# Attention scores in a fixed order, PSUM pools kept open and normalization on ScalarE in a graph network kernel

## The chip, the cores and the metric

The kernel runs on one core of a Trainium2 chip. A core has five engines with queues of their own: TensorE (PE in the profile; its weight loads are PEld), VectorE (DVE), ScalarE (ACT), GpSimd (POOL) and SyncE (SP, which issues most of the DMAs). They meet only through semaphores. The metric is the device time of one execution in microseconds (us); the kernel before takes 974.41 us in the median of three executions (973.85 to 975.27).

## The reference

Two graph layers run over 625 nodes with 1024 features and 20000 edges, everything in float32. The edge list says for each edge its source, its destination and one of 8 types. Cut to what matters:

```python
# layer 0: attention
h = x @ W                                           # 625 x 1024 x 1024
al, ar = h @ a_l, h @ a_r
e = exp(-leaky_relu(al[src] + ar[dst], 0.1))
rowsum = segment_sum(e, src)
h_prime = segment_sum(e[:, None] * h[dst], src) / (rowsum[:, None] + 1e-5)
x = layernorm(x + elu(h_prime))                     # called x1 below
# layer 1: a relational graph network
u = x @ root + bias
for r in range(8):
    mask = edge_type == r
    mean = segment_sum(x[src] * mask, dst) / max(segment_sum(mask, dst), 1)
    u = u + mean @ weight[r]
z = concat([u, x]) @ w_gate + b_gate
x = layernorm(x + tanh(u) * z + x * (1 - z))
```

## The kernel before

**Tiles.** The nodes lie in 5 tiles of 125 rows (`ST`, `TN`). The 1024 features are 8 chunks of 128 (`KC`) where they are summed over, and two halves of 512 columns (`HALF`) where they are produced; one bank of PSUM, the memory that TensorE writes to, is used as 128 rows of 512 float32, and the kernel uses 8 banks.

**The stages**, with the time of each in the profile. First (to 101 us) h = x @ W (ph, L782), while the edges are turned into a dense count matrix for each type: VectorE builds one-hot tiles (L808), TensorE multiplies them (pc, L832), and ScalarE casts the counts (L837) into cj, one tile of source nodes j after the other. From DRAM the counts come back later, type by type (cd, cs, cf).

From about 101 to 140 us the attention scores are made. For a tile j, `all_types` adds the counts of the 8 types (c, L845, L847, L849). `scores_of` makes e = exp(-leaky_relu(al + ar)) times the count: L865 adds, L868 multiplies by 1 where there is an edge, L869 is the leaky ReLU, L870 the exp on ScalarE, L871 the product with the count, L872 the row sum. `turn_scores` transposes e on TensorE (patt, L883) and copies it to attT (L885), the weights of the matrix product with h (phh, L684), which `gather_h` issues and which sums over all five j.

After that (to 167.6 us) `attend` takes each finished row tile of phh: ELU by three operations on ScalarE (L1068 to L1070) and two on VectorE (L1072, L1073), the statistics (L1076, L978), the reciprocal standard deviation on GpSimd (L980 adds the epsilon, L981 is the power) and the normalization on VectorE (L1078). The normalized x1 goes to DRAM, and `turned_pieces` transposes it (px, L673).

**Dense products in pieces.** Every large product after that runs in float32r (0.227 us from one matmul of 128x512 to the next, against 0.86 for one in float32), on three pieces per operand that together carry float32's digits: `prepare` splits a chunk of weights into g, e (ScalarE, L998, L999), m and the final e (VectorE, L1000, L1001); `pieces_of` splits the turned activations into h (ScalarE, L1009), l and d (VectorE, L1010, L1011). A row tile of a half is 24 matmuls: g with h (L1025) and m with l (L1026) into bank p1, e with d (L1029) into bank p2. Ten buffers (`UNITS`) hold prepared chunks: the 8 of the present half and two of the next. The tiles of a half come one after the other; only tile 0 goes chunk by chunk through all three products, the others first through L1025 and L1026 and then through L1029.

These halves follow each other: root0 (167.6 to 197.7 us), root1 (to 227.06), 16 halves of `weight` (to 844.7, each followed by the product with the counts, pu L1195), and the gate: wgx0, wgx1 (x1's part of w_gate), wgu0, wgu1 (u's part), with u transposed in `turn_u` (L1223) during wgx1, to 960.4 us; then the last normalization and the output. root's sums are added to u by two operations on VectorE (L1112, L1113); u was loaded with the bias beforehand, by ten DMAs of 256 KB. The in-degrees per type, which divide the sums, are added up after root0 (L1134, L1136) and transposed on TensorE (p_ins, L1140).

**What sets the order.** The program gives the work in one order, and a scheduler that plans each engine's queue ahead of time may move an instruction past others where the data allow it. `tc.keep_in_program_order` pins an instruction behind the instruction that its engine was given before. The kernel before doesn't pin the scores. It makes each score depend on the one before it: L874 writes a 1 that comes out of the row sum of score j (`turn`), and L868 of score j + 1 takes that 1 as an operand. PSUM comes from pools: before the scores one of 6 and one of 2 banks, which are closed (`begin.close()`) and replaced by one of 8.

## Time and profile before

| quantity | value |
|---|---|
| median of three executions | 974.41 us (973.85 to 975.27) |
| the profiled execution's own time | 973.86 us |
| its span (first to last instruction) | 972.1 us |
| granted TensorE clock, mean | 0.992 |
| TensorE busy | 945.3 us (97%) |
| VectorE busy | 597.2 us (61%) |
| ScalarE busy | 391.4 us (40%) |
| 101 to 140 us: TensorE busy, granted clock | 31.00 of 39.00 us, 0.91 |
| 101 to 140 us: VectorE busy | 38.05 of 39.00 us |
| 227.1 to 844.7 us: TensorE busy | 617.60 of 617.60 us |
| 931.5 to 960.4 us (wgu1): TensorE busy | 27.92 of 28.90 us |

A line of the timeline gives the start, the length, the engine, the line of the kernel, the output and inputs, the number of records, and in brackets how long the engine had been idle before it and whom it waited for. A line of the waits gives the waiting instruction, the one that released it, the total in us, how often, and the longest. A line of the windows gives the stretch, its length, and for TensorE, its weight loads, VectorE, ScalarE and GpSimd the busy time and the records; then the granted clock, the share of the DMA engines' time and GB/s. A line of the groups gives line, engine, operation, output, inputs, shapes and count, then the total busy time in us and the mean of one in ns, and the idle time ahead of it with its releaser. A float32 matmul has two records.

### The profile page before, as it was taken

The numbers are of one execution on the slowest core, as the hardware profiler recorded it, in microseconds if no ns is written. First come the engines' busy times: TensorE is split into PE (matmuls) and PEld (weight loads), VectorE is DVE, ScalarE is ACT, GpSimd is POOL, SyncE is SP. The second block draws the span as 40 slices with busy tenths as digits, with TensorE's granted clock in tenths as the row PEclk, the third lists the DMA queues.
The fourth block names the chain that finished last, engine by engine and source line by source line (L and its number), as shares of the span: only waits on it lengthen the run. The fifth ranks groups of instructions, "written<-read, shape, count | busy, mean of one in ns | idle before, by whom it ended". The sixth has DMA issues, their size and how long they took to land.

```text
span 972.1 us, 10853 instructions
## 1 busy us (share of the span) xinstructions
PE 945.3 (97%) x4075; PEld 730.5 (75%) x4075; DVE 597.2 (61%) x960; ACT 391.4 (40%) x714; POOL 39.5 (4%) x69
## 2 busy tenths in 40 slices
PE   7999699999999999999999999999999999999995
PEld 3555445878888888888888888888888888888874
DVE  1998978976626546356265364562653644639995
ACT  1333837244434515515434345244342551433422
POOL 3000001000000000000000000000000000002123
PEclk9999999999999999999999999999999999999998
DMA  8134862442103113021122120320320211432213
GB/s 298 44 78 102 198 197 75 141 155 87 65 22 121 45 42 108 21 80 66 55 87 63 59 87 23 99 76 11 121 66 22 87 37 50 139 112 74 87 39 112
DMA packets 61631, 83.89 MB, mean 86 GB/s; under 512 B 29323, under 2 KB 29735, under 8 KB 61572
## 3 DMA queue, kind: packets, MB, share of 16 engines
q1 hardware_dynamic: 61364, 82.93, 27.6%
q8 instruction: 34, 0.56, 0.2%
q14 instruction: 25, 0.20, 0.1%
q0 software_dynamic: 208, 0.19, 0.1%
HBM read 71.36 MB, written 11.75 MB: 86 GB/s over the span
## 4 chain that ended last, share of the span: by engine, by line
PE 92%; DVE 5%; ACT 1%; DMA 1%; SPq 0%; issue 0%; POOL 0%; POOLq 0%; DVEq 0%; ACTq 0%
PE pu L1195 19%; PE p_w L1026 15%; PE p_w L1025 15%; PE p_w L1029 15%; PE ph L782 7%; PE phh L684 3%; PE p_root L1029 2%; PE p_root L1025 2%; PE p_wgx L1029 2%; PE p_wgx L1026 2%; PE p_wgx L1025 2%; PE p_root L1026 2%; PE pc L832 2%; PE p_wgu L1029 1%; PE p_wgu L1026 1%; PE p_wgu L1025 1%
## 5 line engine op out<-in xcount | busy, mean ns | idle before, releaser
L1026 PE MATMUL p_w<-m_w,x_l 128*128 128x512 f32 x640 | 249.1, 389 | 0.0
L1025 PE MATMUL p_w<-g_w,x_h 128*128 128x512 f32 x640 | 249.0, 389 | 0.0
L1195 PE MATMUL pu<-y,cf 125*128 125x512 f32 x800 | 184.4, 389 | 0.0
L1177 DVE SCALAR_TENSOR_TENSOR v<-p_w,v 125x512 f32<-125x512 f32 x80 | 55.2, 690 | 201.7 <-PE p_w L1029 153.0
L1029 PE MATMUL p_w<-e_w,x_d 128*128 128x512 f32 x640 | 176.4, 389 | 0.0
L1195 PEld LDWEIGHTS pu<-y,cf 125*128 125x128 f32 x800 | 150.2, 188 | 31.6
L1029 PEld LDWEIGHTS p_w<-e_w,x_d 128*128 128x128 f32 x640 | 120.1, 188 | 25.5 <-DVE e_w L1001 0.3
L1025 PEld LDWEIGHTS p_w<-g_w,x_h 128*128 128x128 f32 x640 | 120.2, 188 | 25.1
L1026 PEld LDWEIGHTS p_w<-m_w,x_l 128*128 128x128 f32 x640 | 120.1, 188 | 25.1 <-DVE m_w L1000 0.2
L1176 ACT ACTIVATE v<-p_w 125x512 f32<-125x512 f32 x80 | 47.6, 595 | 214.0 <-PE p_w L1026 214.0
L1000 DVE SCALAR_TENSOR_TENSOR m_w<-raw_w,e_w 128x512 fp32r<-128x512 f32 x128 | 84.9, 684 | 36.3 <-ACT e_w L999 36.3
L1180 DVE TENSOR_TENSOR y<-v,y 125x512 fp32r<-125x512 f32 x80 | 55.3, 691 | 50.8 <-ACT y L1179 50.8
L998 ACT ACTIVATE g_w<-raw_w 128x512 fp32r<-128x512 f32 x128 | 73.2, 621 | 29.8 <-PE p_w L1025 20.7
L1001 DVE TENSOR_TENSOR e_w<-g_w,m_w 128x512 fp32r<-128x512 f32 x128 | 84.9, 684 | 0.5
L1179 ACT CAST y<-v 125x512 fp32r<-125x512 f32 x80 | 49.2, 615 | 75.1 <-DVE v L1177 75.1
L782 PE MATMUL ph<-w,xT 128*125 128x512 f32 x160 | 77.6, 612 | 0.3 <-ACT xT L714 0.3
L999 ACT ACTIVATE e_w<-raw_w 128x512 fp32r<-128x512 f32 x128 | 73.2, 623 | 0.0
L1199 DVE SCALAR_TENSOR_TENSOR L_gnn_bias_dram_u<-pu,inv,L_gnn_bias_dram_u 125x512 f32<-125x512 f32 x80 | 55.5, 743 | 0.5
L1161 ACT CAST cf<-cs 128x640 fp32r<-128x640 f16 x40 | 25.9, 724 | 54.8 <-PE pu L1195 46.2
L1242 POOL TENSOR_TENSOR L_gnn_bias_dram_u<-L_gnn_bias_dram_u,xr 125x512 f32<-125x512 f32 x10 | 17.4, 1743 | 744.2 <-ACT L_gnn_bias_dram_u L1227 712.0
L684 PE MATMUL phh<-h_sb,attT 125*125 125x512 f32 x100 | 45.9, 614 | 0.4 <-ACT attT L885 0.4
L782 PEld LDWEIGHTS ph<-w,xT 128*125 128x125 f32 x160 | 27.9, 192 | 24.1 <-issue 22.2
(159 smaller groups left out, 972.0 us busy)
## 6 DMA issues: line engine op xcount, KB each, us to landing
raw_w<-in_L_gnn_weight_dram SPq DMA_DIRECT2D x64, 512.0 KB
cd<-cj SPq DMA_DIRECT2D x40, 160.0 KB
cs<-cd SPq DMA_DIRECT2D x8, 800.0 KB
x<-in_x_dram SPq DMA_DIRECT2D x8, 512.0 KB
w<-in_L_gnn_W_dram SPq DMA_DIRECT2D x8, 512.0 KB
raw_root<-in_L_gnn_root_dram SPq DMA_DIRECT2D x8, 512.0 KB
raw_wgx<-in_L_gnn_w_gate_dram SPq DMA_DIRECT2D x8, 512.0 KB
raw_wgu<-in_L_gnn_w_gate_dram SPq DMA_DIRECT2D x8, 512.0 KB
```

Source lines behind the costliest of these rows:

```text
L684: nc.tensor.matmul(banks_h[t, half][:n, :], attT[:nj, j, tile_cols(t)], h_sb[:nj, j, half * HALF:(half + 1) * HALF], start=(j == 0), stop= ...
L782: nc.tensor.matmul(p[:n, :], xT[:, k, :n], w0_sb[k][:, half * HALF:(half + 1) * HALF], start=k == 0, stop=k == KC - 1)
L998: nc.scalar.activation(g, w, AF.Copy, scale=DOWN)
L999: nc.scalar.activation(e, w, AF.Copy, scale=UP12 * DOWN)
L1000: nc.vector.scalar_tensor_tensor(m, w, UP12, e.bitcast(F32), op0=OP.mult, op1=OP.subtract)
L1001: nc.vector.tensor_tensor(e, g.bitcast(F32), m.bitcast(F32), op=OP.subtract)
L1025: nc.tensor.matmul(p1, h[:, k, :], g, start=k == 0, stop=False, skip_group_check=True)
L1026: nc.tensor.matmul(p1, l[:, k, :], m, start=False, stop=k == KC - 1, skip_group_check=True)
L1029: nc.tensor.matmul(p2, d[:, k, :], e, start=k == 0, stop=k == KC - 1, skip_group_check=True)
L1180: nc.vector.tensor_tensor(lo[:n], v[:n], hi[:n].bitcast(F32), op=OP.subtract)
L1195: nc.tensor.matmul(p, c[:m, t, j * 128:(j + 1) * 128], piece[:m], start=(t == 0 and i == 0), stop=(t == ST - 1 and i == 1), skip_group_che ...
L1199: nc.vector.scalar_tensor_tensor(at, p[:n], inv[:n, j, r:r + 1], at, op0=OP.mult, op1=OP.add)
```

## The change

- The scores are pinned on VectorE (`in_turn`) in an order that the program gives; `turn` is gone. `scores_of` is split, so that the product with the counts (`times_edges`) and the row sum (`sum_scores`) have places of their own. Scores 0 and 1 are begun in `first_scores` as soon as al and ar are there. The types of tiles 3 and 4 are added between the scores, and the copy of score 0's transposes lies on VectorE. The m pieces of root's first 8 chunks are pinned behind the scores.
- Two PSUM pools of 6 and 2 banks stay open for the whole kernel. A bank that names no pool takes them in turn, six and two; `begin.close()` is gone. patt and the phh of tile 3 name the pool of 2; px of x, p_count, p_edges, pc and p_ar that of 6.
- x1 is normalized on ScalarE: a [125, 1] operation on VectorE (-mean), one on ScalarE (times the reciprocal deviation) and one Identity over 1024 columns with both as pointers. The epsilon is added on VectorE, not on GpSimd. px of x1's tile 0 is issued after two of the five phh of tile 4.
- `dense_tiles` takes the last two row tiles of a half together, chunk by chunk, in root0, root1, wgx0, wgx1 and wgu0 (`goes_on`).
- root's p1 is evicted on ScalarE into u, and p2 added on VectorE. The ten bias loads are gone; the bias is added in relation 1, by five adds on VectorE after one load of 256 KB per half.
- The in-degrees are added in float16, in place of iota, and turned after root1 by five float16 matmuls with a float16 identity; one operation on VectorE takes the place of five. Relation 0's counts are loaded and cast after root1.
- `turn_u` of u's tiles 3 and 4 moves from wgx1 to wgu0, behind its tiles 0 and 1.

Where the diff shows only added lines, the lines that they replace are in the listing above.

```diff
...
     rawp = ctx.enter_context(tc.tile_pool(name="f_raw", bufs=4, side="right"))
-    begin = ExitStack()
-    ps = [begin.enter_context(tc.tile_pool(name="f_ps0", bufs=6, space=bass.MemoryType.PSUM))]
-    ps_h = begin.enter_context(tc.tile_pool(name="f_ps_h", bufs=2, space=bass.MemoryType.PSUM))
-    def bank(name):
-        return ps[0].tile([128, 512], F32, tag="bank", name=name)
+    ps = [ctx.enter_context(tc.tile_pool(name=f"f_ps{n}", bufs=n, space=bass.MemoryType.PSUM)) for n in (6, 2)]
+    turns = []
+    def bank(name, pool=None):
+        if pool is None:
+            pool = len(turns) % 8 // 6
+            turns.append(name)
+        return ps[pool].tile([128, 512], F32, tag="bank", name=name)
+    def in_turn(ins):
+        tc.keep_in_program_order(ins)
...
+        def all_types(j, part, put=lambda ins: None):
...
+            if part == 0:
+                c4 = attp.tile([128, ST, 4, 128], F16, name="c4")[:, :, :, :n]
+                fours.append(c4)
+                put(nc.vector.tensor_tensor(c4, cjs[j][:, :, 0:4, :n], cjs[j][:, :, 4:8, :n], op=OP.add))
+                return
+            c4 = fours.pop()
...
+            c1 = attp.tile([128, ST, 128], F16, name=f"c1_{j}")[:, :, :n]
+            ct.append(c1)
+            put(nc.vector.tensor_tensor(c2, c2, c4[:, :, 2:4, :], op=OP.add))
+            put(nc.vector.tensor_tensor(c1, c2[:, :, 0, :], c2[:, :, 1, :], op=OP.add))
...
+        def scores_of(j, parts=(0, 1)):
...
+            if 0 in parts:
+                e = attp.tile([128, ST, 128], F32, name=f"e_{j}")[:, :, :n]
+                es.append(e)
+                in_turn(nc.vector.tensor_tensor(
+                    e, ar_b[:, j * 128:j * 128 + n].unsqueeze(1).to_broadcast([128, ST, n]),
+                    al.unsqueeze(2).to_broadcast([128, ST, n]), op=OP.add))
+                in_turn(nc.vector.scalar_tensor_tensor(e, ct[j], 1.0, e, op0=OP.min, op1=OP.mult))
+            if 1 in parts:
+                in_turn(nc.vector.scalar_tensor_tensor(es[j], es[j], SLOPE, es[j], op0=OP.mult, op1=OP.max))
+                nc.scalar.activation(es[j], es[j], AF.Exp, scale=-1.0)
+        def times_edges(j):
+            in_turn(nc.vector.tensor_tensor(es[j], es[j], ct[j], op=OP.mult))
+        def sum_scores(j):
+            in_turn(nc.vector.tensor_reduce(rsum[:, :, j], es[j], axis=AX.X, op=OP.add))
...
+                p = bank(f"patt_{j}_{t0}", 1)
...
+                if j:
+                    nc.scalar.copy(attT[:n, j, c0:c1], p[:n, :c1 - c0])
+                else:
+                    in_turn(nc.vector.tensor_copy(attT[:n, j, c0:c1], p[:n, :c1 - c0]))
...
         def counted(j):
-            all_types(j, cjs[j])
+            if j < ST - 2:
+                all_types(j, 0)
+                all_types(j, 1)
...
+        def first_scores(_):
+            spread_ar()
+            scores_of(0)
+            scores_of(1, parts=(0,))
+            times_edges(0)
+            scores_of(1, parts=(1,))
...
                     if steps == n_steps:
-                        due.append((i + 6, lambda _: spread_ar(), None))
-                        due.extend((max(i + 6 + 4 * j, (j + 1) * NG + LAG), lambda _: es.append(scores_of(len(es))), None)
-                                   for j in range(AHEAD))
+                        due.append((i + 6, first_scores, None))
...
+            sum_scores(j)
             if j + 1 < ST:
+                later_types = j + 3 if j < 2 else None
+                if later_types:
+                    all_types(later_types, 0, in_turn)
+                times_edges(j + 1)
+                if later_types:
+                    all_types(later_types, 1, in_turn)
+                if j + 2 < ST:
+                    scores_of(j + 2)
...
         rstd = small.tile([128, 1], F32, name="rstd")
-        nc.gpsimd.tensor_scalar(rstd[:n], mv[:n, 1:2], EPS, None, op0=OP.add)
+        nc.vector.tensor_scalar(rstd[:n], mv[:n, 1:2], EPS, None, op0=OP.add)
...
             nc.scalar.activation(e, w, AF.Copy, scale=UP12 * DOWN)
-            nc.vector.scalar_tensor_tensor(m, w, UP12, e.bitcast(F32), op0=OP.mult, op1=OP.subtract)
+            rest = nc.vector.scalar_tensor_tensor(m, w, UP12, e.bitcast(F32), op0=OP.mult, op1=OP.subtract)
+            if pinned:
+                in_turn(rest)
...
+    def dense_tiles(ts, chunks, name, by_chunk):
+        sums = {t: (bank(f"p1_{name}_{t}"), bank(f"p2_{name}_{t}")) for t in ts}
+        def first(t, k, g, m):
+            h, l, _ = x1[t]
+            nc.tensor.matmul(sums[t][0], h[:, k, :], g, start=k == 0, stop=False, skip_group_check=True)
+            nc.tensor.matmul(sums[t][0], l[:, k, :], m, start=False, stop=k == KC - 1, skip_group_check=True)
+        def second(t, k, e):
+            nc.tensor.matmul(sums[t][1], x1[t][2][:, k, :], e, start=k == 0, stop=k == KC - 1, skip_group_check=True)
...
+            for t in ts:
+                first(t, k, g, m)
+                if by_chunk:
+                    second(t, k, e)
+        if not by_chunk:
...
+                for t in ts:
+                    second(t, k, e)
+        return sums
+    def dense(name, put, after=None, goes_on=False, whole=False):
...
+        steps = [(t,) for t in range(ST - 2)] + ([(ST - 2, ST - 1)] if goes_on else [(ST - 2,), (ST - 1,)])
+        for ts in steps:
+            for t, (p1, p2) in dense_tiles(ts, chunks, name, ts[0] == 0 or len(ts) > 1).items():
+                n = 128 if whole else rows_of(t)
+                put(t, p1[:n, :], p2[:n, :])
+                if t == 1:
+                    prepare(UNITS - KC)
+                if after:
+                    after(t)
...
         mv, rstd = rstd_of(stats, n)
-        nc.vector.tensor_scalar(x_t[:n], x_t[:n], mv[:n, 0:1], rstd[:n], op0=OP.subtract, op1=OP.mult)
+        shift = small.tile([128, 1], F32, name="shift")
+        nc.vector.tensor_scalar(shift[:n], mv[:n, 0:1], -1.0, None, op0=OP.mult)
+        nc.scalar.activation(shift[:n], shift[:n], AF.Copy, scale=rstd[:n])
+        nc.scalar.activation(x_t[:n], x_t[:n], AF.Identity, scale=rstd[:n], bias=shift[:n])
...
-    prepare(KC)
+    prepare(KC, pinned=True)
...
     done = [attend(0)]
-    turned_pieces(done[0], 0, "x1")
...
         gather_h(EARLY + 1, j)
+        if j == 1:
+            turned_pieces(done[0], 0, "x1")
...
     l1p = ctx.enter_context(tc.tile_pool(name="f_l1", bufs=1))
-    u = start_rows(l1p, bias, ("u0", "u1"))
+    u = [[l1p.tile([128, HALF], F32, tag=f"u{h}_{t}", name=f"u{h}_{t}") for h in range(2)] for t in range(ST)]
...
+    def start_u(h):
+        def put(t, p1, p2):
+            at = u[t][h]
+            nc.scalar.activation(at, p1, AF.Copy, scale=1.0 + EPS12)
+            nc.vector.scalar_tensor_tensor(at, p2, -EPS12, at, op0=OP.mult, op1=OP.add)
+        return put
...
-    dense("root0", add_to(u, 0), after=later_x1)
+    dense("root0", start_u(0), after=later_x1, goes_on=True, whole=True)
...
+    ins = iota16[:R]
+    ident16 = src2.rearrange("p b g h w -> p (b g h w)")[:R, :R]
+    def add_ins():
+        nc.vector.tensor_copy(ident16, ident[:R, :R])
+        nc.vector.tensor_tensor(ins, ins16[:, 0, :], ins16[:, 1, :], op=OP.add)
+        for t in range(2, ST):
+            nc.vector.tensor_tensor(ins, ins16[:, t, :], ins, op=OP.add)
+    in_p = yp.tile([TN, 1], F32, name="in_p")
+    def use_ins():
+        p = bank("p_ins")
+        for t in range(ST):
+            nc.tensor.matmul(p[:TN, t * R:(t + 1) * R], ins[:, t * 128:t * 128 + TN], ident16, start=True, stop=True)
+        p = p[:TN, :ST * R]
+        nc.vector.tensor_scalar(inv[:TN].rearrange("p t r -> p (t r)"), p, 1.0, None, op0=OP.max)
+        nc.vector.reciprocal(inv, inv)
+        nc.vector.tensor_reduce(in_p, p, axis=AX.X, op=OP.add)
+    def sum_ins():
+        p = bank("p_all")
+        nc.tensor.matmul(p[:1, :1], in_p, ones[:TN, :1], start=True, stop=True)
+        nc.vector.tensor_scalar(astray, p[:1, :1], -1.0, float(E), op0=OP.mult, op1=OP.add)
...
+    dense("root1", start_u(1), goes_on=True, whole=True)
+    add_ins()
+    use_ins()
...
     cast_counts(0)
-    dense("root1", add_to(u, 1))
...
-            dense(f"w{r}_{h}", put)
+            dense(f"w{r}_{h}", put, after=lambda t: (r, h, t) == (0, 0, 1) and sum_ins())
...
+                    if r == 1:
+                        nc.vector.tensor_tensor(at, at, bias_row[:n], op=OP.add)
+            if r == 1:
+                bias_row = l1p.tile([128, HALF], F32, tag="v", name=f"bias_{h}", bufs=2)
+                nc.sync.dma_start(bias_row, bass.AP(tensor=bias.tensor, offset=bias.offset + h * HALF,
+                                                    ap=[[0, 128], [1, HALF]]))
...
-    dense("wgx0", add_to(z, 0))
-    dense("wgx1", add_to(z, 1), after=turn_u)
-    dense("wgu0", mix(0))
+    dense("wgx0", add_to(z, 0), goes_on=True)
+    dense("wgx1", add_to(z, 1), after=lambda t: t < ST - 2 and turn_u(t), goes_on=True)
+    dense("wgu0", mix(0), after=lambda t: t < 2 and turn_u(t + ST - 2), goes_on=True)
```

## The prediction

> **What bounds the kernel now.** I read the page's totals and chain first, then the waits of TensorE, then its timeline and the windows where it is not full.
>
> ```profile
> span 972.1 us, 10853 instructions
> PE 945.3 (97%) x4075; PEld 730.5 (75%) x4075; DVE 597.2 (61%) x960; ACT 391.4 (40%) x714; POOL 39.5 (4%) x69
> PE 92%; DVE 5%; ACT 1%; DMA 1%; SPq 0%; issue 0%; POOL 0%; POOLq 0%; DVEq 0%; ACTq 0%
> ...
> PE patt L883 <- DVE e L871: 7.6, 3, 4.9
> PE p_wgu L1029 <- DVE e_wgu L1001: 1.0, 2, 0.6
> PE phh L684 <- ACT attT L885: 0.4, 1, 0.4
> ```
>
> TensorE is busy for 97%, so only its idle or slow stretches can be won. The largest wait that this change touches is that of patt (the turned scores): three times, 7.6 us, longest 4.9. The timeline of TensorE and four windows of 10 us show the place:
>
> ```profile
> 104.09 4.92 PE L832 MATMUL pc<-m_hot,s_hot 128*128 128x240 f16 x42
> 111.51 0.78 PE L883 MATMUL patt<-ident,e 125*125 125x125 f32 x5 [2.50 <-DVE e L871]
> 112.69 1.98 PE L684 MATMUL phh<-h_sb,attT 125*125 125x512 f32 x4 [0.40 <-ACT attT L885]
> 119.56 1.41 PE L883 MATMUL patt<-ident,e 125*125 125x125 f32 x5 [4.89 <-DVE e L871]
> 120.76 7.22 PE L684 MATMUL phh<-h_sb,attT 125*125 125x512 f32 x12
> 128.36 5.32 PE L684 MATMUL phh<-h_sb,attT 125*125 125x512 f32 x12
> 139.58 0.78 PE L883 MATMUL patt<-ident,e 125*125 125x125 f32 x5 [0.21 <-DVE e L871]
> ...
> 100.00:110.00 10.00, 9.01 (x75) 6.66 (x73) 9.12 (x15) 9.66 (x22) 0.00 (x0) 1.00 0.73 186
> 110.00:120.00 10.00, 3.20 (x11) 1.73 (x12) 10.00 (x15) 9.97 (x21) 0.95 (x1) 0.89 0.83 172
> 120.00:130.00 10.00, 10.00 (x26) 5.05 (x26) 10.00 (x19) 4.86 (x10) 0.00 (x0) 0.77 0.90 289
> 130.00:140.00 10.00, 9.79 (x30) 4.56 (x29) 9.93 (x17) 2.20 (x4) 0.00 (x0) 1.00 0.63 197
> ```
>
> From 110 to 140 VectorE (third busy figure) is full, while TensorE idles 2.50 + 0.40 + 4.89 + 0.21 = 8.0 us. A second loss: the granted clock falls to 0.77, and the same 12 records take 7.06 us, from 120.76 to the next patt at 127.82, against 5.15 later; with patt's 1.20 against 0.54 that is 2.6 us. VectorE is full because 20 operations on root's pieces stand between the scores: these two rows, 10 of each from 117.5 to 138.6, at one per 0.60 us, so 12.0 us.
>
> ```profile
> L1001 DVE TENSOR_TENSOR e_root<-g_root,m_root 128x512 fp32r<-128x512 f32 x16 | 10.8, 688 | 0.0
> L1000 DVE SCALAR_TENSOR_TENSOR m_root<-raw_root,e_root 128x512 fp32r<-128x512 f32 x16 | 10.5, 688 | 0.2 <-ACT e_root L999 0.2
> ...
> L1078 DVE TENSOR_SCALAR x<-x,mv,rstd 125x1024 f32<-125x1024 f32 x5 | 4.1, 812 | 3.8 <-POOL rstd L981 3.8
> L1266 ACT ACTIVATE gnn_b_gate_dram_y<-gnn_b_gate_dram_y,shift,rstd 125x512 f32<-125x512 f32 x8 | 6.1, 808 | 22.5 <-POOL shift L1262 22.5
> ...
> 930.00:940.00 10.00, 9.63 (x43) 7.34 (x42) 9.80 (x16) 3.24 (x6) 3.14 (x2) 1.00 0.14 46
> 940.00:950.00 10.00, 9.39 (x42) 7.45 (x41) 9.43 (x16) 0.63 (x1) 2.95 (x6) 1.00 0.09 27
> ```
>
> The last two lines are the gate stage: VectorE above 94%, TensorE short by 1.0 us. Between 227.06 and 844.7 TensorE is full in every window: nothing to win there.
>
> **1. Scores in fixed order.** A score costs VectorE five operations of 0.72 to 0.87, ScalarE an exp of 0.73. The fixed order puts root's pieces behind the last score. The types' sum of node tile j=3 (1.38 + 0.72 + 0.40 = 2.5 us) moves in between, so VectorE saves 12.0 - 2.5 = 9.5 us there. Walked operation by operation with these durations, 0.12 us from engine to engine: ar_b is copied by 104.6 as before; score 0 leaves its lrelu at 107.3, exp 108.1 (behind ScalarE's casts), product 109.7. patt 0 starts at 109.8, 0.8 after the last pc (109.01), not 2.5. Its copy now lies on VectorE, where it is next in line: phh from 111.1. Product 1 is ready at 114.15 and TensorE comes for it at 114.56; product 2 at 120.7 against 121.1; product 3 at 126.08, a stall of 0.24; product 4 at 130.1. So patt 4 starts at 130.3, not 139.58: **-9.3 us**. The same phh lie ahead of it in both orders. The margins are 0.3 to 0.4 us, so this term is -6 if each product is some 0.8 us later than walked, and -9.6 at best, when the stall of 0.24 goes too. The clock's 2.6 us is inside the 9.3: the longest idle left is about 0.8, and the trace's 0.40 and 0.21 are followed by nothing slow.
>
> The Trainium skill, "TensorE: Matmul & The Clock Gate", section "HAM oscillation", says that idle gaps above about 3.4 us halve the clock; the row agrees (4.89 idle, then 0.77), and by it as by the rows the short gaps left keep the full clock.
>
> **2. From x1 to root0.** Root's 16 pinned pieces now follow the scores, from 131 to 146 on VectorE, and the other 4 among the attends. phh takes 17.2 us as before, px 0 is due at 151.4. x1's path grows: rstd's add on VectorE (0.17, the row of the 125x1 operations) for POOL's 0.31, pow 0.57, two operations on ScalarE instead of one on VectorE. The 1024-wide Identity is not in the trace: at least 0.81 (the 512-wide row above), at most 1.62 (twice). I take 1.2: attT's copies give 0.47 at 375 columns and 0.37 at 250, 0.8 ns a column, so 0.81 + 0.4. Queued behind it on ScalarE are the next tile's q and m, and behind those VectorE's adds. By the walk x_0 is ready at 150.0 for px 0 at 151.4; x_3 at 168.6 for 170.1; x_4 at 175.0 for 176.4. Before, x_3 and x_4 had 8.4 and 3.3 us. So **0**, with 0.7 to 1.4 us of cover; gone, each px costs its lateness, together 0 to +4.
>
> The Trainium skill, "ScalarE: Activation LUTs", section "Rules for kernel authors", speaks against the move: add and mul belong on VectorE. The rows give 0.81 there and an estimated 1.2 here, but VectorE is the busier engine (8.4 to 9.7 of 10 from 150 to 190, ScalarE 1.7 to 7.1). By the page's rule each tile would be 0.4 later, all inside its cover; by the rows VectorE gains 5 x 0.72 us.
>
> **3. The last two tiles together.** In root0 the pair begins at 177.25 and asks for l_4 0.9 later; by the walk VectorE has it at 179.3: **+1.15**, between 0 and +3. In the gate stage each chunk is freed 1.36 us after the previous one during the last 10.9 us, instead of all in the last 5.4, so the next half's pieces are ready before it starts. The four halves take 115.7 us (844.72 to 960.4), against 113.2 for 20 tiles of 24 matmuls at 0.227 us and five turns of 0.87. Of the excess 2.4 (1.7 of it in wgu1) I take **-1.8**; 0 to -2.4 if it works, up to +3 if the eight operations of u's last two turns, now in wgu0, crowd VectorE: u_4's pieces are walked ready 12 to 17 us into wgu0, asked for at 18.1.
>
> **4. In-degree sums.** root1 takes 29.3 us from 197.73 to 227.06 with p_ins (5 x 0.33 by its neighbours' starts) and p_all between, against 27.2 for 120 matmuls of 0.227. fp16 needs one pass: 0.6 at the end, p_all goes under w0. **-1.2**, between 0 and -1.8.
>
> **5. At nothing.** Ten bias loads of 256 KB leave SP's queue at 167 to 172.5, where only x1's stores and weight loads stand behind them; two return in r=1. Ten adds of 0.60 in r=1 lie under 38.6 us halves in which VectorE is 55 to 60% busy. Evicting p1 on ScalarE frees 0.6 per tile; nobody waits for it while a bank is free. Two pools of 6 and 2 banks rotate as one of 8 did: 0, or up to +2 if phh waits for a bank. Tail: rstd's add off POOL, **-0.2**.
>
> **Sum.** -9.3 + 1.15 - 1.8 - 1.2 - 0.2 = -11.35 on the profiled 973.86 (span 972.1 and 1.8 around it): 962.5. The median 974.41 stands 0.55 above that run, so 963.0. A measurement here can tell about 0.2% (2 us) from no change.
>
> **Rivals.** (a) *VectorE just misses.* It is full from 105 to 180 and the covers are 0.3 to 1.4 us; if they fail, scores give -7 and px and the joint tiles cost +2.5 more: 968. For it: the thin margins. Against: the rows repeat within 1%. (b) *The gate stage turns worse*, +3 instead of -1.8: 968. For it: VectorE at 94 to 98%. Against: the work per half is the same. (c) *Nothing comes of it*: the scores are held by something other than VectorE's order, such as ScalarE, 9.97 busy from 110 to 120: 974. Against: its 4.86 and 2.20 after. (d) *Slower: x1's path through ScalarE.* m, q and Identity wait in one queue, each behind VectorE's adds, and five px wait for it in turn. It decides when each is over 2.5 us late beyond its cover (5 x 2.65 outweighs 11.35 and 2 us): that is four more ScalarE operations of 0.6 to 0.7 ahead of each. At 3.2 us each: +16 - 11.35, 979. For it: q waits for x on VectorE for 3.0 us already. Against: in root0 ScalarE is 17 to 22% busy.
>
> **Chances.** Forecast 0.55 (961 to 966), (a) 0.22, (b) 0.08, (c) 0.04, (d) 0.11. Faster 0.85, same 0.04, slower 0.11. Low end: no stall in root0, -9.3 - 1.8 - 2.4 - 0.2 = -13.7, 960.7. The high end takes in (a) and (b) with the 2 us for banks and a stall more: 971.
>
> **What would show it.** Right: patt 4 near 130, no wait of patt above 1 us, granted clock 1.00 in 110 to 130, W from about 217, wgu1 below 27.5 us. Wrong: TensorE waiting for e, for x (px) or for l and d of root's last tiles by more than 2 us in all, or for wgu's pieces; a clock below 0.9 there.

## The result and the profile after

The changed kernel takes 970.12 us in the median (969.66 to 970.68, five executions), the kernel before 974.43 (973.85 to 975.27, five executions): a ratio of 0.9955, interval 0.9941 to 0.997. It is faster by 4.3 us, where 11.4 were forecast. The page's totals and its chain, of the kernel after:

```profile
span 968.0 us, 10885 instructions
PE 945.6 (98%) x4075; PEld 730.1 (75%) x4075; DVE 596.6 (62%) x964; ACT 405.6 (42%) x732; POOL 36.5 (4%) x59
PE 87%; DVE 8%; ACT 2%; issue 1%; POOL 1%; DMA 0%; SPq 0%; DVEq 0%; POOLq 0%; ACTq 0%
```

TensorE is busy for 945.6 us, against 945.3 before, although several microseconds of slow and idle time are gone: some of its work has become longer. The waits of TensorE after (engine, who waits, for whom, total in us, times, longest):

```profile
PE px L680 <- DMA x<-in_x_dram: 5.0, 1, 5.0
PE p_count L746 <- DVE less L730: 1.0, 1, 1.0
PE p_root L1052 <- DVE x_l L1036: 0.9, 1, 0.9
PE patt L891 <- DVE e L880: 0.6, 1, 0.6
PE phh L691 <- DVE attT L896: 0.5, 1, 0.5
PE p_root L1055 <- DVE x_d L1037: 0.5, 1, 0.5
```

The waits for scores fell from 7.6 to 0.6 us, those for wgu's pieces from 1.0 to none, and the pair of root0 waits for 1.4 in all. Waits are where the forecast said they would be. TensorE's timeline and the windows, after:

```profile
109.81 0.81 PE L891 MATMUL patt<-ident,e 125*125 125x125 f32 x5 [0.60 <-DVE e L880]
111.14 3.67 PE L691 MATMUL phh<-h_sb,attT 125*125 125x512 f32 x8 [0.51 <-DVE attT L896]
114.64 0.71 PE L891 MATMUL patt<-ident,e 125*125 125x125 f32 x5
121.20 0.71 PE L891 MATMUL patt<-ident,e 125*125 125x125 f32 x5
126.03 0.76 PE L891 MATMUL patt<-ident,e 125*125 125x125 f32 x5
130.07 0.75 PE L891 MATMUL patt<-ident,e 125*125 125x125 f32 x5
```

```profile
110.00:120.00 10.00, 9.49 (x30) 4.73 (x30) 9.90 (x14) 9.93 (x21) 0.01 (x1) 1.00 0.69 173
120.00:130.00 10.00, 10.00 (x32) 4.67 (x30) 9.62 (x14) 4.15 (x9) 0.94 (x1) 1.00 0.71 261
930.00:940.00 10.00, 10.00 (x46) 8.27 (x45) 9.76 (x15) 0.00 (x0) 2.54 (x2) 1.00 0.18 51
940.00:950.00 10.00, 10.00 (x46) 8.29 (x45) 9.35 (x19) 2.59 (x4) 5.47 (x8) 1.00 0.26 79
```

The last patt starts at 130.07 (forecast 130.3), 9.5 us earlier than before; 1.7 us of that are already there at the first patt (109.81 against 111.51). The clock is 1.00 in all these windows, and in the gate TensorE is full while VectorE is at 94 to 98%. So the gain arrived where it was expected. To see where it went, the span is cut at three points of TensorE's timeline: W's first matmul (L1025 before, L1051 after), wgx0's first, and the end of TensorE's last record.

| stretch | before | after | difference |
|---|---|---|---|
| start to W | 227.06 | 217.82 | -9.24 |
| the 16 halves of W | 617.66 | 623.10 | **+5.44** |
| gate, to TensorE's end | 115.83 | 113.51 | -2.32 |
| TensorE's end to the span's end | 11.55 | 13.57 | **+2.02** |
| span | 972.1 | 968.0 | -4.1 |

Two stretches lost 7.5 us. The first is one group of TensorE, before (L1195) and after (L1249); the columns are the total busy time in us, the mean of one record in ns, and the idle time before:

```profile
L1195 PE MATMUL pu<-y,cf 125*128 125x512 f32 x800 | 184.4, 389 | 0.0
```

```profile
L1249 PE MATMUL pu<-y,cf 125*128 125x512 f32 x800 | 189.8, 396 | 0.0
```

TensorE waits for nothing there; the same 800 matmuls simply take longer, 5.4 us in all, while the groups of the dense products beside them keep their mean of 389 ns. The diff doesn't touch these matmuls, but it moves one of their operands: the first tile of `y`, the moving operand, begins at byte 48928 of its SBUF partition where it began at 49024 (addresses as the compiled kernels have them; the traces don't show addresses). Two edits of the in-degree sums make the 96 bytes, by a count of the tiles in both kernels: `in_r`, which had four buffers of 32 bytes ahead of y, is gone (-128), and the column `in_p` has come into y's own pool (+32). The second loss is on the way from TensorE's end to the last store. VectorE and ScalarE after:

```profile
955.49 0.69 DVE L1308 SCALAR_TENSOR_TENSOR gnn_b_gate_dram_y<-xr,gnn_b_gate_dram_y 125x512 f32<-125x512 f32 x1
958.36 0.69 DVE L1310 TENSOR_TENSOR u<-p_wgu,u 125x512 f32<-125x512 f32 x1 [2.18 <-ACT u L1309]
```

```profile
956.29 1.52 ACT L1326 ACTIVATE gnn_b_gate_dram_y<-gnn_b_gate_dram_y,shift,rstd 125x512 f32<-125x512 f32 x2 [3.52 <-POOL shift L1322]
957.71 0.61 ACT L1309 ACTIVATE u<-u 125x512 f32<-125x512 f32 x1
```

The same wait of VectorE before:

```profile
962.44 0.69 DVE L1250 TENSOR_TENSOR L_gnn_bias_dram_u<-p_wgu,L_gnn_bias_dram_u 125x512 f32<-125x512 f32 x1 [1.46 <-ACT L_gnn_bias_dram_u L1249]
```

VectorE now waits 2.18 us for L1309, a scaling of u that needs nothing from TensorE and could have run at any time, but stands on ScalarE behind the normalization of tile 3 (L1326), which waits for GpSimd. Before, the wait was 1.46 and began 0.43 us behind TensorE's end; now it begins 1.75 behind it. TensorE's gain in the gate left VectorE's elementwise work behind, and the two differences make the 2.0 us.

### The profile page after: what moved, and what is told of

The parts are those of the page before. It is cut to its first block, busy times and chain, and to the rows that moved or that the text cites. A ratio compares the mean times of both kernels' runs of the same rounds, so it can differ in the third digit from the quotient of the medians.

```text
span 968.0 us, 10885 instructions
## 1 busy us (share of the span) xinstructions
PE 945.6 (98%) x4075; PEld 730.1 (75%) x4075; DVE 596.6 (62%) x964; ACT 405.6 (42%) x732; POOL 36.5 (4%) x59
## 4 chain that ended last, share of the span: by engine, by line
PE 87%; DVE 8%; ACT 2%; issue 1%; POOL 1%; DMA 0%; SPq 0%; DVEq 0%; POOLq 0%; ACTq 0%
PE pu L1249 19%; PE p_w L1051 15%; PE p_w L1052 15%; PE p_w L1055 15%; PE ph L789 7%; PE p_wgx L1052 2%; PE p_wgx L1055 2%; PE p_wgx L1051 2%; PE pc L839 2%; PE p_root L1052 1%; PE p_root L1055 1%; PE p_root L1051 1%; PE p_wgu L1051 1%; PE p_wgu L1055 1%; PE p_wgu L1052 1%
## 5 line engine op out<-in xcount | busy, mean ns | idle before, releaser
L1051 PE MATMUL p_w<-g_w,x_h 128*128 128x512 f32 x640 | 249.2, 389 | 0.0
L1249 PE MATMUL pu<-y,cf 125*128 125x512 f32 x800 | 189.8, 396 | 0.0
L1249 PEld LDWEIGHTS pu<-y,cf 125*128 125x128 f32 x800 | 150.6, 188 | 36.4
L1051 PEld LDWEIGHTS p_w<-g_w,x_h 128*128 128x128 f32 x640 | 120.1, 188 | 25.2
L1253 DVE SCALAR_TENSOR_TENSOR u<-pu,inv,u 125x512 f32<-125x512 f32 x80 | 55.6, 741 | 5.2 <-PE pu L1249 5.2
L844 ACT CAST cj<-pc 128x480 f16<-128x480 f32 (+1 forms) x55 | 27.8, 557 | 41.2 <-PE pc L839 41.2
```

What stands on the lines that cost most here:

```text
L1051: nc.tensor.matmul(sums[t][0], h[:, k, :], g, start=k == 0, stop=False, skip_group_check=True)
L1249: nc.tensor.matmul(p, c[:m, t, j * 128:(j + 1) * 128], piece[:m], start=(t == 0 and i == 0), stop=(t == ST - 1 and i == 1), skip_group_che ...
L1253: nc.vector.scalar_tensor_tensor(at, p[:n], inv[:n, j, r:r + 1], at, op0=OP.mult, op1=OP.add)
```

## The experiments

The start of the kernel differs between executions: the first patt lies between 109.4 and 111.9 us in the profiles of kernels that leave everything ahead of it alone. Where medians lie within 2 us of each other, the stretches inside the profiles are compared as well. Ratios are to the kernel before as it ran beside each experiment; its medians there lie between 974.95 and 975.67 us.

**The place of y.** The first theory was that y has to begin at a multiple of 64 bytes (e1); the other half of the test puts the kernel *before* off its place (e2).

```diff
-    in_p = yp.tile([TN, 1], F32, name="in_p")
+    in_p = yp.tile([TN, 16], F32, name="in_p")[:, :1]
```

> The changed kernel with one edit: the column in_p, which lies in SBUF just ahead of y, is allocated 64 bytes wide instead of 4 (it takes 32 as it is), so that y's tiles begin at a multiple of 64 bytes, as they do in the kernel before; in the changed kernel they begin 32 past one. Theory A (the pace of pu's matmuls hangs on where the moving operand y begins): pu's records go from 0.396 back to 0.389 us, each of the 16 halves of W is 0.36 us shorter, the whole 5.8 us shorter: 964.3. Theory B (pu is slower because of the two PSUM pools, or because VectorE or ScalarE now do other work beside it): pu stays at 0.396 and the time at 970.1.

```diff
     inv = yp.tile([128, ST, R], F32, name="inv")
+    yp.tile([128, 8], F32, name="shim")
```

> The kernel before with one edit: a tile of 32 bytes that nothing uses is allocated ahead of y, so that y begins 32 bytes past a multiple of 64. Theory A (where y begins sets pu's pace): pu at 0.396 us, 800 matmuls x 0.0072 = 5.8 us longer, 980.2. Theory B (the pools, or the work beside pu): no change, 974.4.

The kernel before slows to 979.53 us, ratio 1.0047 (1.0033 to 1.0061), by nothing but 32 unused bytes, and its 16 halves take 622.26 us instead of 617.66: that y's place costs some 4.6 us there is shown. But y at 48960 gains nothing beyond 0.4 us (969.78, ratio to the kernel before 0.9947, 0.9934 to 0.9961; the 16 halves take 622.66): a multiple of 64 is not the rule. pu in the first and in the second:

```profile
L1249 PE MATMUL pu<-y,cf 125*128 125x512 f32 x800 | 189.2, 394 | 0.0
```

```profile
L1196 PE MATMUL pu<-y,cf 125*128 125x512 f32 x800 | 189.2, 395 | 0.0
```

Then y was put back where it had been, at 49024, with the changed kernel otherwise whole (e5):

```diff
-    in_p = yp.tile([TN, 1], F32, name="in_p")
+    in_p = yp.tile([TN, 32], F32, name="in_p")[:, :1]
```

> The changed kernel with in_p allocated 128 bytes wide, so that y begins at a multiple of 128 bytes, at the very address that it has in the kernel before. Theory A2 (pu's pace hangs on y's place within 128 bytes, not within 64): records of 0.389 us, the 16 halves of W 617.7 us instead of 623.1, the whole 5.0 to 5.5 us shorter than the changed kernel: 964.8. Theory B (pu is slow in the changed kernel because of the two pools or of the work beside it; moving y in the kernel before cost the same by chance): 0.394 and 970 as in the kernel with y at 64.

964.16 us (963.92 to 965.93), ratio 0.989 (0.9873 to 0.9907), and the 16 halves take 617.86:

```profile
L1249 PE MATMUL pu<-y,cf 125*128 125x512 f32 x800 | 184.4, 389 | 0.0
```

Of the 7.1 us that were missing, 5.2 are here, in the 16 halves; the medians, from two sessions, differ by 6.0. The rule in mind by then, a multiple of 128, was tried 128 bytes further (e9: `in_p` of 64 columns, y at 49152):

> The changed kernel with in_p 256 bytes wide: y begins at another multiple of 128 bytes, 128 further than in the kernel before. Theory A2 (only the place within 128 bytes counts): pu's records at 0.389 us, 964. If it were that one address: 0.394, 970.

It fell: 967.63 in one execution, and

```profile
L1249 PE MATMUL pu<-y,cf 125*128 125x512 f32 x800 | 188.5, 394 | 0.0
```

What remained were two rules that the old address meets and 49152 doesn't: an odd multiple of 128, or a distance of a multiple of 256 bytes from `cf`, the stationary operand, at 77184. Widening cf's tile moves it down; y stays or moves with it (one execution each). e13 has the edit below on e5's kernel, e14 on e9's; e15 leaves cf and moves y to 49280 (`in_p` of 96 columns); e16 widens cf by 24 columns instead of 32, on the changed kernel itself.

```diff
-        c = aggp.tile([128, ST, SP], F32R, tag="cf", name=f"cf_{r}")
+        c = aggp.tile([128, ST * SP + 32], F32R, tag="cf", name=f"cf_{r}")[:, :ST * SP].rearrange("p (t s) -> p t s", t=ST)
```

> The kernel of e5 (y at 49024) with cf, the stationary operand of pu, 128 bytes lower: 77056, an even multiple of 128, where it was 77184, an odd one. Theory absolute (y itself has to be an odd multiple of 128): pu stays at 389 ns, 184.4 us in all, span 962. Theory relative (y and cf have to be a multiple of 256 apart; here they are 28032, which is 128 more than one): pu 393 to 396 ns, 188.5 to 190, span 967.

> The kernel of e9 (y at 49152, pu 394 ns) with cf 128 bytes lower, at 77056: both even multiples of 128, 27904 = 109 x 256 apart. Relative: pu back at 389 ns, 184.4 us, span 962. Absolute: 394 ns as in e9, 188.5 us, span 966.

> The kernel of e5 with y another 256 bytes further, at 49280, an odd multiple of 128 and 109 x 256 from cf, which stays at 77184. Absolute and relative alike: pu 389 ns, 184.4 us, span 962. If only the old address 49024 works: 394 ns, 188.5 us, span 966.

> The changed kernel itself (y at 48928, pu 396 ns) with cf 96 bytes lower, at 77088, so that the two are 110 x 256 apart, neither on a multiple of 128. Relative, and nothing else: pu 389 ns, 184.4 us, span 962 to 963. If a multiple of 128 is wanted for itself: 393 to 396 ns as before this edit, span 967 to 968.

pu in the four, in this order:

```profile
L1249 PE MATMUL pu<-y,cf 125*128 125x512 f32 x800 | 188.5, 395 | 0.0
```

```profile
L1249 PE MATMUL pu<-y,cf 125*128 125x512 f32 x800 | 184.4, 390 | 0.0
```

```profile
L1249 PE MATMUL pu<-y,cf 125*128 125x512 f32 x800 | 184.4, 390 | 0.0
```

```profile
L1249 PE MATMUL pu<-y,cf 125*128 125x512 f32 x800 | 184.2, 390 | 0.0
```

The times of these four are 969.66, 966.2, 965.0 and 964.58 us. Moving cf alone makes the fast kernel slow; moving it after y makes the slow one fast; and in the last, the changed kernel with y untouched at 48928, neither operand lies on a multiple of 64, and it is fast. All nine placements agree with one rule, the distance (the tiles of y and the columns of cf that a matmul takes all lie multiples of 256 from the first):

| y | cf | cf - y, modulo 256 | mean record of pu, ns |
|---|---|---|---|
| 49024 (before, e5) | 77184 | 0 | 389 |
| 49152 (e14) | 77056 | 0 | 390 |
| 49280 (e15) | 77184 | 0 | 390 |
| 48928 (e16) | 77088 | 0 | 390 |
| 48928 (after) | 77184 | 96 | 396 |
| 48960 (e1) | 77184 | 64 | 394 |
| 49056 (e2) | 77184 | 224 | 395 |
| 49152 (e9) | 77184 | 128 | 394 |
| 49024 (e13) | 77056 | 128 | 395 |

Without `in_p`, y would begin at 48896 by the count given above, 128 off, and be slow by this rule too; that wasn't run.

A last test of addresses (e11) put `h_sb`, the moving operand of the float32 product phh, on a multiple of 128 (on top of e7, below):

```diff
     heldp = stage.enter_context(tc.tile_pool(name="f_held", bufs=1))
+    heldp.tile([128, 8], F32, name="shim")
```

> The one with y on 128, root0's last tiles one after the other and the early scale, and 32 unused bytes ahead of h, so that h's rows, phh's moving operand, begin at a multiple of 128 bytes instead of 96 past one. If the place within 128 bytes counts for every moving operand as it does for y (7 ns per record): phh's 200 records take 0.6 to 1.4 us less, 960.8. If a float32 matmul, whose record takes 0.43 us for the same 512 columns, doesn't feel it: no change, 961.8.

961.09 us (960.33 to 961.56), no different from e7, and a phh record takes 593 ns in both. The pad moves attT, the stationary operand, along with h, so no distance between the two changes: by the rule above there was nothing to gain. (The tiles begin 20480 bytes apart, a multiple of 256; but the matmuls take attT in steps of 500 and 2500 bytes, so nearly all of them are off one already.) Whether float32 matmuls follow the rule wasn't tried.

**The tail.** On e1's kernel (e3), the scaled difference of u's last tile is made two tiles earlier, into a tile of its own:

```diff
+            if (t, h) == (ST - 3, 1):
+                last, low = difference(ST - 1, 1), l1p.tile([128, HALF], F32, tag="v", name="low", bufs=2)
+                nc.scalar.activation(low[:rows_of(ST - 1)], last[1], AF.Copy, scale=-EPS12)
+                early.append((*last, low[:rows_of(ST - 1)]))
...
-                nc.scalar.activation(th, th, AF.Copy, scale=-EPS12)
-                nc.vector.tensor_tensor(th, p2, th, op=OP.mult)
-                nc.vector.tensor_tensor(at, at, th, op=OP.add)
+                nc.vector.tensor_tensor(low, p2, low, op=OP.mult)
+                nc.vector.tensor_tensor(at, at, low, op=OP.add)
```

> The first of these kernels, and the scaled difference of u's last tile (ScalarE, times -EPS12) is made two tiles earlier into a tile of its own. Theory C (the end is longer because ScalarE holds that operation behind tile 3's normalization, which waits for GpSimd's shift): VectorE's idle 2.2 us before the last product with p2 goes, the time from TensorE's end to the span's end falls from 13.6 to 11.5 us, the whole 2.1 us shorter than the first: 962.2. Theory D (VectorE is late with its own work at the end, and the wait only covers that): less than 0.5 us shorter.

968.29 us (966.93 to 970.23), ratio 0.9929 (0.9916 to 0.9943). From TensorE's end to the end of VectorE's last operation it takes 5.95 us, where e1 takes 8.1: the wait of 2.18 is gone. The median moves by 1.5 only, and the ranges overlap; this profile has a loss elsewhere, in root0, to which the runs on root0's pair return.

The rival explanation of the lost tail was that wgu0's joint tiles merely push VectorE's work later. On e1's kernel wgu0's last two tiles come one after the other again (e4):

```diff
-    dense("wgu0", mix(0), after=lambda t: t < 2 and turn_u(t + ST - 2), goes_on=True)
+    dense("wgu0", mix(0), after=lambda t: t < 2 and turn_u(t + ST - 2))
```

> The first of these kernels, but wgu0's last two tiles one after the other as before. Theory E (what taking them together gains on TensorE is given back, since VectorE is full from wgu0 to the end): TensorE waits up to 1.7 us in wgu1 again, the time from its end to the span's end is about 1.7 us shorter, and the time stays within 0.6 us of the first. Theory F (the gain is real and the end has a cause of its own): 1.5 to 2 us slower than the first.

```profile
PE p_wgu L1055 <- DVE e_wgu L1027: 1.5, 2, 0.9
```

970.56 us (969.89 to 971.89): no different from e1. TensorE waits again for the pieces, and the tail to VectorE's last operation falls from 8.1 to 5.63 us. What joint tiles save in wgu0 is lost behind it as long as the tail waits for VectorE. The same edit on e7, where the tail's wait is gone (e12), asks whether anything is left of it:

> The one with y on 128, root0's last tiles one after the other and the early scale, and wgu0's last tiles one after the other too. Theory E (VectorE is full from wgu0 to the end, so what TensorE gains there is given back): TensorE waits some 1.5 us in wgu1, its end comes that much later, VectorE's end within 0.6 us of the same: 961.8. Theory F (the gain is real, now that ScalarE's wait at the end is gone): 963.5.

962.17 us (961.55 to 962.67) against e7's 961.81: the gate takes 115.69 us to TensorE's end instead of 113.52, the tail to VectorE's last operation 4.62 instead of 5.94. Of 2.2 us saved, 0.9 reach the end in these two profiles, too little for the medians to tell.

**root0's pair.** On e5, root0's last two tiles one after the other (e6: `goes_on` left out there):

> As the one with y on 128, but root0's last two tiles one after the other. Theory G (taking them together costs root0 two waits of 0.7 to 0.9 us for the pieces of the last x1 tile, and in some executions a drop of the granted clock to 0.5 for some 3 us behind them): both waits go, the clock stays 1.00 there, 1.4 us shorter than the one with y on 128, 2.7 where the clock had dropped: 963.0. Theory H (the waits only move, since root1's first chunks are then prepared later): no change, 964.8.

963.03 us (962.55 to 964.18), ratio 0.9871 (0.9856 to 0.9886), against 0.989. The two waits of 0.9 and 0.5 are gone, and from the last patt to W it takes 85.97 us instead of 87.70. The intervals overlap, so the profile carries this one. The pair can cost more than its waits. In e3's profile, with the same pair (waits of 0.7 and 0.9 us), the windows show

```profile
180.00:182.00 2.00, 1.04 (x4) 0.56 (x4) 2.00 (x6) 0.70 (x2) 0.00 (x0) 1.00 0.14 45
182.00:184.00 2.00, 2.00 (x5) 1.63 (x6) 1.67 (x3) 0.08 (x1) 0.00 (x0) 0.52 0.01 3
184.00:186.00 2.00, 2.00 (x7) 1.54 (x7) 0.56 (x1) 1.71 (x3) 0.00 (x0) 0.63 0.00 0
```

The granted clock halves behind the pair: 12 matmuls in 4 us where e5 has 21 in the same two windows. e4 shows the same (0.50 and 0.77); the changed kernel and e5 don't (1.00), with waits within 0.2 us of these. The traces show where they differ. Within a profile, all changes of the granted clock lie a whole number of steps of 3.41 us apart. In e3 and e4 the clock is 0.5 for one such step, which is 1.7 us lost; in the kernel before it was 0.5 for two, from 117.75 on. Both waits of e3, and both of e4, fall into one step, in which TensorE is busy for 54% of the time, and the next one runs at half the clock. In the changed kernel and in e5 the two waits lie in different steps, the emptier one busy for 78 and 75%. Where the limit lies isn't shown: with both waits in one step at 60 and 61% (e13, e15) the clock held, and in the kernel before a step with 44% (from 107.5) cost nothing.

From the last patt to p_ins e3 and e4 take 89.2 us, the profiles with the pair's waits and a full clock 87.3 to 88.0. It may be why e3's times spread over 3.3 us: its two longest executions, the profiled one among them, have a mean granted clock of 0.994, the other three 0.996.

All that helped together, e6 with the early scaling (e7):

> y on 128, root0's last tiles one after the other, and the scaled difference of u's last tile made early. If the three add up: 5.2 + 1.4 + 2.0 us below the changed kernel's 970: 961.4, and the time from TensorE's end to the span's end 11.5 to 12 us. If VectorE's own lateness sets the end (theory D): 963.

```profile
951.14 0.68 DVE L1323 TENSOR_TENSOR low<-p_wgu,low 125x512 f32<-125x512 f32 x1
954.48 1.00 DVE L1341 TENSOR_SCALAR gnn_b_gate_dram_y<-gnn_b_gate_dram_y,mv,rstd 125x512 f32<-125x512 f32 x2 [0.69 <-POOL rstd L1005]
```

961.81 us (959.86 to 962.53), ratio 0.9854 (0.9836 to 0.9872). L1323 follows without a gap, and VectorE ends 5.94 us after TensorE, 8.26 in e6. By the medians this version is 8.3 us faster than the changed kernel, which ran in another session, and 13.4 us faster than the kernel before, which took 975.17 beside it.

**x1's normalization.** On e5, back on VectorE (e8), one operation instead of three:

```diff
-        shift = small.tile([128, 1], F32, name="shift")
-        nc.vector.tensor_scalar(shift[:n], mv[:n, 0:1], -1.0, None, op0=OP.mult)
-        nc.scalar.activation(shift[:n], shift[:n], AF.Copy, scale=rstd[:n])
-        nc.scalar.activation(x_t[:n], x_t[:n], AF.Identity, scale=rstd[:n], bias=shift[:n])
+        nc.vector.tensor_scalar(x_t[:n], x_t[:n], mv[:n, 0:1], rstd[:n], op0=OP.subtract, op1=OP.mult)
```

> As the one with y on 128, but x1 normalized by one operation on VectorE as before. The prediction's step 2 (the move to ScalarE costs nothing while it stays inside its cover, and VectorE gains 5 x 0.72 us): with the operation back on VectorE the last x1 tiles come up to 1 us later or earlier, root0's waits change by less than 1 us, the whole within 1 us of the one with y on 128. The Trainium skill's rule (add and mul belong on VectorE): 0.4 us per tile earlier, root0's waits for the last tile shorter by that, 0.5 to 1 us shorter.

967.75 us (966.34 to 968.23), ratio 0.9917 (0.9902 to 0.9931): 3.6 us slower than e5. VectorE, TensorE and the windows:

```profile
178.56 0.68 DVE L1037 SCALAR_TENSOR_TENSOR x_d<-x_l,x_h 128x512 fp32r<-128x512 f32 x1
179.68 0.81 DVE L1108 TENSOR_SCALAR x<-x,mv,rstd 125x1024 f32<-125x1024 f32 x1 [0.44 <-POOL rstd L1005]
```

```profile
180.59 1.12 PE L680 MATMUL px<-ident,x 128*128 128x128 f32 x8 [2.58 <-issue]
```

```profile
180.00:182.00 2.00, 1.41 (x10) 1.34 (x11) 1.80 (x4) 0.74 (x2) 0.00 (x0) 0.87 0.38 109
182.00:184.00 2.00, 2.00 (x6) 1.59 (x5) 2.00 (x4) 0.89 (x2) 0.00 (x0) 0.50 0.45 152
```

The normalization of the last tile ends at 180.49, and px starts 0.1 later, after 2.58 us of idleness (the profile says "issue"; VectorE's row shows what ended just then). Then the clock falls to 0.87, 0.50 and 0.78 in three windows of 2 us: again one step of 3.41 us at 0.5, from 181.48 on, behind a step in which TensorE was busy for 26%; 1.7 us lost. The two waits of root0's pair go in exchange, and from the last patt to p_ins e8 takes 89.7 us, e5 87.3. So 2.4 of the 3.6 are shown in the profiles; the rest lies ahead of the last patt, where executions differ anyway. VectorE is busy without a gap from 165 us until shortly before L1108, so the way through ScalarE, longer for a tile by itself, is the shorter one for the kernel.

**root's pieces between the scores.** On e5, the m pieces of root are no longer pinned behind the scores (e10):

```diff
-    prepare(KC, pinned=True)
+    prepare(KC)
```

> As the one with y on 128, but the m pieces of root's first 8 chunks are not pinned, and the planner puts 3 operations on root's pieces ahead of score 2's product, 7 ahead of score 3's and 10 ahead of score 4's. The prediction's step 1 (those operations are what the scores wait for, 0.60 us each): patt of score 2 some 1.4 us late, of score 3 some 4, patt 4 at 136 instead of 130; 5.8 us slower than the one with y on 128, 970, and up to 2.6 more where the granted clock drops behind the waits. Rival (the order of the scores among themselves is what counts, not the pieces): 964.

965.52 us (965.17 to 966.81), ratio 0.9905 (0.9888 to 0.9921): 1.4 us, not 5.8. VectorE does put ten of the pieces' operations among the scores, where the old kernel had twenty, and the last product ends at 134.7, where e5 has it at 129.5:

```profile
133.88 0.80 DVE L880 TENSOR_TENSOR e<-e,c 128x625 f32<-128x625 f32 x1
```

```profile
129.43 0.78 PE L891 MATMUL patt<-ident,e 125*125 125x125 f32 x5 [0.58 <-DVE e L880]
130.55 5.41 PE L691 MATMUL phh<-h_sb,attT 125*125 125x512 f32 x12 [0.34 <-ACT attT L894]
135.81 0.71 PE L891 MATMUL patt<-ident,e 125*125 125x125 f32 x5
```

But TensorE is given 48 phh records ahead of the last patt instead of 40, and waits for 0.6 us at most. From patt 0 to px 0 of x1 it takes 2.7 us longer; of that, 1.35 come back, since root0's pair no longer waits. So the pieces do make a score late (the last product by 4.6 us counted from patt 0, for ten operations of 0.60), but TensorE fills part of that with other work.

## Why the prediction was wrong

The direction was right; the forecast of 963.0 us and the measured 970.12 differ by 7.1, and two terms account for it, both in step 5.

**The step that failed is step 5, "At nothing", together with the sentence that W's stretch has "nothing to win".** A full TensorE was taken for a fixed time. Step 5 listed bias loads, adds, evictions and banks, and weighed nothing of what the new and the missing tiles do to the addresses of the operands. They moved y by 96 bytes against cf, worth +5.4 us over 800 matmuls. That is the largest missing term: with the distance at a multiple of 256 again the 16 halves take 617.75 to 617.96 us (e5, e14, e15, e16), against 617.66 before and 623.10 in the changed kernel.

**The tail in step 5, -0.2, measured +2.0.** Of the epsilon's 0.2, 0.1 is there (from the end of the last aggregate to the normalization 0.94 us, before 1.05), but L1309 behind tile 3's normalization is 2.18 us late. Step 3 was right about TensorE (-1.8 forecast, -2.3 in the table) and didn't ask what is late next: the same 94 to 98% of VectorE that made rival (b) possible moved the loss behind TensorE's end. By the profiles of e7 and e12, 0.9 us of what the pair in wgu0 saves TensorE reach the end, and that only with the tail's wait gone.

The measured 970.12 lies inside the stated range, up to 971, but by luck: that end was made of rivals (a) and (b) and of stalls for a bank, and none of them came.

Point by point, the rest:

- **Step 1, -9.3: right in size.** Products 2, 3 and 4 end at 120.6, 125.9 and 129.9, walked as 120.7, 126.1 and 130.1; the last patt is 9.5 us earlier than before. 1.7 us of it lie ahead of the first patt, which moves by up to 2.5 us between executions, so part of it may be luck. The reason given is open in part. The sum charged the 12 us of pieces to the scores one for one; e10 gives ten of the twenty their places back, and the kernel loses 1.4 us. How much of the rest comes from the other ten, from the chain through `turn` that is gone, or from what TensorE has to do meanwhile isn't shown: neither the chain alone nor all twenty were tried.
- **Step 2, 0: right.** No px of x1 waits. The Identity takes 1.23 us (estimated 1.2), x_0 is ready at 150.0 as walked, x_4 at 175.85 instead of 175.0, with 0.5 us of cover left of the 1.4. Costed as "0" it hid what the step protects: without it (e8) the median is 3.6 us higher, 2.4 of it shown in the profile. The rule weighed there, from the Trainium skill, "ScalarE: Activation LUTs", section "Rules for kernel authors", would have kept the operation on VectorE; on a VectorE that is already full the measurement decides against it.
- **Step 3 in root0, +1.15:** 1.35 of waits, and sometimes the clock.
- **Step 4, -1.2:** start to W was forecast at -9.3 + 1.15 - 1.2 = -9.35 and is -9.24; p_ins takes 0.45 us instead of five times 0.27.
- **Rivals.** (a) and (b) named times near 968 and didn't happen; (d) has its sign reversed by e8, and its counter-argument, ScalarE 17 to 22% busy, holds for 170 to 190 us only (38% over the whole of root0); (c) is out by the scores.
- **The clock.** The forecast that short gaps keep the full clock held in the changed kernel. The figure of about 3.4 us for one gap (the Trainium skill, "TensorE: Matmul & The Clock Gate", section "HAM oscillation") is no safe bound for this case: e8 lost the clock behind a gap of 2.58 us, e3 and e4 behind gaps of 0.7 and 0.9, for 3.41 us each time.

## What to carry to other kernels

A stretch in which TensorE is full isn't a constant: compare the mean of each matmul group before and after, and when a tile enters or leaves a pool, look at which operands it moves, since 7 ns on each of 800 matmuls were worth more than any wait left in this kernel. Follow a gain past the engine that bounds the kernel to the last store, and ask of every operation in the tail whether it could have been done earlier. The cost of an engine's extra work depends on whether the waiting engine has other work to do in the meantime (e10), and the right engine for an operation is the one with room, not the one that is faster at it (e8).

## What the runs showed of the hardware

- The records of a float32r matmul of 125x512 take 389 to 390 ns in the mean (800 in 184.2 to 184.4 us) when its moving and its stationary operand begin a multiple of 256 bytes apart in SBUF, and 394 to 396 (800 in 188.5 to 189.8 us) when they don't (64, 96, 128 and 224 bytes off; nine placements). Whether either of them begins on a multiple of 64 or 128 didn't matter. Why this is so the profiles don't show; the weight loads themselves take 187 to 188 ns in both cases.
- Within a profile, the changes of the granted clock lie a whole number of steps of 3.41 us apart (277 of them between the two changes of the kernel after). It fell to 0.5 for one step behind a step in which TensorE was busy for 26% (e8, a single gap of 2.58 us) or 54% (e3 and e4, two gaps of 0.7 and 0.9 us), and held behind steps with 60 to 78% in the same place. So whether a given pair of waits costs clock seems to depend on where it falls among the steps, which differs between executions. In the kernel before it fell inside the gap of 4.89 us, for two steps. The busy share alone doesn't decide it: one step with 44% (kernel before, from 107.5 us) cost nothing.
